# Third experts: rows fetched four tiles ahead, tile 0's small operations moved into the attention, eight buffers for scatter addresses and output weights

## The chip, the cores and the metric

One core of one Trainium2 chip runs the whole program in one launch. The metric is device time in microseconds; the time of a kernel is the median of its runs.

## The reference

The program is a network of four layers on an image of 256 channels and 64 x 64 = 4096 places (tokens), in float32. Layer 0 is a convolutional attention over boxes, layer 1 a deformable convolution, layer 2 a linear attention followed by a mixture of experts, layer 3 a full softmax attention followed by a mixture of experts. The change lies in the code of the two mixtures, which are called second experts (layer 2) and third experts (layer 3) here. The third one, cut to what is computed:

```python
gate_logits = xf @ Wg + bg                       # 4096 tokens, 8 experts
top_w, top_i = jax.lax.top_k(gate_logits, 2)
top_w = jax.nn.softmax(top_w, axis=-1)
w_dense = jnp.sum(one_hot(top_i, 8) * top_w[..., None], axis=1)
for e in range(8):
    h = jax.nn.gelu(xf @ W1[e] + b1[e])          # 256 -> 1024
    out = out + w_dense[:, e:e + 1] * (h @ W2[e] + b2[e])
```

The second mixture has the same form with a hidden size of 256.

## The kernel before

**Routing.** Each token goes to two experts only. `route` (L2028) handles a block of 512 tokens: it normalises them, computes logits, picks the two experts, counts, finds for each token its place in the list of each of its experts, and scatters the token's row of 260 numbers (256 channels, its number, its two weights, its first expert) by POOL's indirect DMAs into `xs` in memory (L2117, eight DMAs a block). `full_table` (L2125) and `tile_table` (L2157) then cut the lists into tiles of 256 rows: for each tile the expert, the first row, and masks. In layer 3 the first 20 tiles are taken from the counts before the last block (table A), and the other 16 from the final counts (table B). Three more tiles can follow under an If on a counter.

**One tile of experts** (`expert_tiles`, L2269):

- `load` calls `expert_load` (L2219): SP reads the tile's expert and first row from the table into registers and issues three DMAs: the rows of `xs` into `f_x` (260 KB; L2229 or L2235), and the two weight matrices (L2231, L2233). It runs `ahead` tiles before use: three in the second experts, two in the third. `f_x` has `ahead + 3` buffers.
- `turn` calls `expert_turn` (L2238): PE transposes the rows into PSUM (L2241), DVE copies them to `f_xT` (L2242).
- `where` (L2320) makes from the four extra numbers of each row the scatter addresses `f_at` and the weights `f_wgt` by nine small DVE operations (L2325 to L2333), each on two columns. Its five tags have four buffers each, so the `f_at` of a tile is written over the one of four tiles before, which a scatter may still be reading.
- `first` (L2296): PE's products into `f_h_ps` by the helper `mm` (L152), ACT's gelu into `f_h` (L2303).
- In the third experts `sides` (L2336) forms differences of the second weights on POOL (L2344), and `seven` (L2347) computes the second product as seven smaller ones, with DVE's sums around them (`f_hs` L2351 to L2354, `f_u` and `f_y` L2369 to L2373).
- `second` (L2375): DVE adds the bias to `f_y` (L2379 in the third experts, L2384 in the second), ACT scales it by `f_wgt` (L2386), and two POOL indirect DMAs scatter it to `ys` at the addresses in `f_at` (L2387). It is emitted one tile after `first`.

The loop at L2408 to L2422 emits, for tile i: the load of tile i + ahead, `first` of i, `turn` and `where` of i + 1, `second` of i - 1.

**The attention of layer 3** (`attn3`, L2483) runs over 8 blocks of 512 queries with 16 pairs of key tiles each. A round is `scores` (L2647: seven products on PE at L2653, DVE's sums of them at L2658 and in `together` at L2640 to L2643, ACT's exponential L2672, DVE's differences L2676 to L2678) and `values` (L2681, PE L2692) of two rounds before. Between rounds of a block stand the steps of the block before it: `finish` (L2701: the last product, DVE's `t` L2708) and the five steps of `route`. In the last block `full_table` and the `expert_load` of tile 0 are emitted in its round 9 (L2766 to L2770), and `expert_turn` of tile 0 in round 14 of 0 to 15 (L2771). The steps of the last block itself (four `finish`, five of `route`, then `tile_table`) are run inside the third experts' first tiles: `finish` between products of tile 0, the scatter into `xs` in tile 2, the table in tile 3.

**What sets the order.** Within `attn3` the order of PE and POOL is written out by hand; in the third experts that of PE, until the steps are used up. Everything else (DVE, ACT and SP in these stretches, and all engines in the second experts) is ordered by a scheduler when the program is built: it may move an operation of `where` of a later tile in front of one of an earlier tile. Each engine executes its list in order. A read of rows of `xs` that is emitted after a scatter into `xs` waits for that scatter.

Of the kernel before, what the change touches and what calls it, by code (L numbers as in the profile page):

```python
# [10 lines left out]
F32 = mybir.dt.float32  # L11
BF16 = mybir.dt.bfloat16
I32 = mybir.dt.int32
# [6 lines left out]
P = 128  # L20
C = 256
# [71 lines left out]
class Net:  # L93
# [30 lines left out]
    def weights(self, pool, names):  # L124

        for i, name in enumerate(names):
            src = self.A[name].rearrange("(k p) n -> p k n", p=P)
            w = pool.tile(list(src.shape), F32, tag=name, name=name)
            eng = self.nc.sync if i % 2 == 0 else self.nc.scalar
            eng.dma_start(out=w, in_=src)  # L130
            self.w[name] = w

    def rows(self, pool, first, last):

        lo, hi = PR[first].start, PR[last].stop
        pr = pool.tile([P, hi - lo], F32, tag=f"pr_{first}", name="pr", bufs=1)
        self.nc.scalar.dma_start(out=pr, in_=self.A["pr"][lo:hi].partition_broadcast(P))
        for name, at in PR.items():
            if lo <= at.start and at.stop <= hi:
                self.r[name] = pr[:, at.start - lo : at.stop - lo]  # L140
# [2075 lines left out]
            part = off[:, i : i + k, :].rearrange("p i k -> p (i k)")  # L2216
            nc.vector.scalar_tensor_tensor(part, self.nth[:, : k * NI], float(2 * N), part, ALU.add, ALU.mult)

    def expert_load(self, S, tab, j, x, w1, w2, rows_first):  # L2219
        nc, A, L = self.nc, self.A, S["L"]  # L2220
        why = "worked out from counts of tokens"
        e = nc.values_load(tab[0:1, 0, j : j + 1], engines=[mybir.EngineType.SP], min_val=0, max_val=(NE - 1) * P,
                           skip_runtime_bounds_check_because=why)
        row = nc.values_load(tab[0:1, 1, j : j + 1], engines=[mybir.EngineType.SP], min_val=0, max_val=NE * N - MT,
                             skip_runtime_bounds_check_because=why)
        src = self.xs[bass.ds(row, MT), :].rearrange("(i p) c -> p i c", p=P)
        x = x()
        if rows_first:
            nc.sync.dma_start(out=x, in_=src)  # L2229
        w1 = w1()  # L2230
        nc.sync.dma_start(out=w1, in_=A[f"f{L}_w1"][bass.ds(e, P), :])  # L2231
        w2 = w2()
        nc.sync.dma_start(out=w2, in_=A[f"f{L}_w2"][bass.ds(e, P), :])  # L2233
        if not rows_first:
            nc.sync.dma_start(out=x, in_=src)  # L2235
        return x, w1, w2

    def expert_turn(self, x, p, xT):  # L2238
        for k in range(2):
# [29 lines left out]
    def expert_tiles(self, S, order, wp, ps, steps, early, pre, written):  # L2269
        nc, A = self.nc, self.A  # L2270
        L = S["L"]
        tiles = range(len(order))
        of = lambda i, nm: S[order[i][0]][nm]
        hidden = 256 if L == 2 else 1024
        KH = hidden // P
        ahead = 3 if L == 2 else 2 if pre or not early else 1

        def load(i):
            if pre and i == 0:
                return pre["tile"]  # L2280
            lent = pre and i % 3 == 0
            pool = pre["pool"] if lent else wp
            kw = dict(bufs=1) if lent else dict(bufs=2) if early else {}
            return self.expert_load(
                S, of(i, "tab"), order[i][1],
                lambda: wp.tile([P, NI, CX], F32, tag="x", name="f_x", bufs=ahead + 3),
                lambda: pool.tile([P, 2 * hidden + KH], F32, tag="w1", name="f_w1", **kw),
                lambda: pool.tile([P, KH * C + C], F32, tag="w2", name="f_w2", **kw),
                i > 0,
            )  # L2290

        def turn(x):
            p = ps.tile([P, 2, MT], F32, tag="x", name="f_x_ps", bufs=1 if early else 2)
            return self.expert_turn(x, p, wp.tile([P, 2, MT], F32, tag="xT", name="f_xT", bufs=3))
# [23 lines left out]
            return h  # L2318

        def where(i, x):  # L2320

            tl = lambda tag, dt=F32: wp.tile([P, NI], dt, tag=tag, name="f_" + tag, bufs=4)
            first, second, to, wgt, at = tl("first"), tl("second"), tl("to"), tl("wgt"), tl("at", I32)
            op, j = nc.vector, order[i][1]
            op.tensor_scalar(first, x[:, :, C + 3], of(i, "ex")[:, j : j + 1], None, ALU.is_equal)  # L2325
            op.tensor_scalar(second, first, -1.0, 1.0, ALU.mult, ALU.add)
            op.tensor_tensor(wgt, second, x[:, :, C + 2], ALU.mult)
            op.tensor_scalar(second, second, float(N), None, ALU.mult)
            op.tensor_tensor(to, x[:, :, C], second, ALU.add)
            op.tensor_tensor(to, to, of(i, "in")[:, j, :], ALU.mult)  # L2330
            op.tensor_tensor(at, to, of(i, "off")[:, j, :], ALU.add)
            op.tensor_tensor(first, first, x[:, :, C + 1], ALU.mult)
            op.tensor_tensor(wgt, wgt, first, ALU.add)  # L2333
            return at, wgt

        def sides(w2):  # L2336

# [58 lines left out]
                    written.close()  # L2396

        nc.scalar.activation(wp.tile([P, 1], F32, tag="g", name="f_gelu", bufs=1), self.one, AF.Gelu)
        ld = {i: load(i) for i in tiles[:ahead]}
        if pre:  # L2400
            for f in pre["ahead"][:1]:
                f()
            xT = pre["xT"]
        else:
            xT = turn(ld[tiles[0]][0])
        to = where(tiles[0], ld[tiles[0]][0])
        done = None
        for i in tiles:  # L2408
            if i + ahead <= tiles[-1]:
                ld[i + ahead] = load(i + ahead)  # L2410
            x, w1, w2 = ld.pop(i)
            h = first(xT, w1, (pre["ahead"][1:] if i == 0 else ()) if steps else None)
            now = (i, h, w2, sides(w2)) + to
            step()
            if i < tiles[-1]:
                xT = turn(ld[i + 1][0])
                to = where(i + 1, ld[i + 1][0])
            if done is not None:
                second(*done)
                step()  # L2420
            done = now
# [61 lines left out]
    def attn3(self, t, S):  # L2483
# [6 lines left out]
        with (  # L2490
# [28 lines left out]
            if True:  # L2519
# [6 lines left out]
                def bank(few=False):  # L2526
                    banks.append(banks.pop(0))
                    return (keep_ps if banks[-1] == "q" else ps).tile([P, NB], F32, tag=banks[-1], name="a3_q_ps")
# [172 lines left out]
                def finish(b, i):  # L2701
                    o = bank()[:, : C + 1]
                    at = oTs[b].rearrange("p m h n -> p m (h n)")[:, :, i * P : (i + 1) * P]
                    self.mm(o, [(at[:, kt, :], wvp[:, kt, :]) for kt in range(2)])
                    ti = b * TPB + i
                    r = S["r"][:, ti : ti + 1]
                    nc.vector.reciprocal(r, o[:, C : C + 1])
                    nc.vector.scalar_tensor_tensor(t[:, ti, :], o[:, :C], r, t[:, ti, :], ALU.mult, ALU.add)  # L2708
# [41 lines left out]
                with tc.manual_schedule(engines={ET.PE, ET.Pool}):  # L2750
                    steps = iter(())
                    for g in range(first, G + LAG):
                        if g < G:
                            scores(g)
                        values(g - LAG)
                        if g + 3 < G:
                            fetch(g + 3)
                        b, j = divmod(g - LAG, NPAIR)
                        if b > 0:
                            if j < TPB:  # L2760
                                finish(b - 1, j)
                            elif j == TPB:
                                steps = route((b - 1) * TPB, TPB)
                            elif j % 2 == 0 or b == NBLK - 1:
                                next(steps, None)
                            if b == NBLK - 1 and j == TPB + 5:  # L2766
                                self.full_table(S, keep, bank)
                                one = lambda shape, tag: keep.tile([P] + shape, F32, tag=tag, name="f_" + tag, bufs=1)
                                tile = self.expert_load(S, S["A"]["tab"], 0, lambda: one([NI, CX], "x"), lambda: one([16 * P + 8], "w1"),
                                                        lambda: one([9 * C], "w2"), True)  # L2770
                            if b == NBLK - 1 and j == NPAIR - 2:  # L2771
                                xT = self.expert_turn(tile[0], bank().rearrange("p (k n) -> p k n", k=2), one([2, MT], "xT"))
            left.close()
            last = route((NBLK - 1) * TPB, TPB)
            go = lambda: next(last, None)
            self.experts(
                S, [go] * 5 + [lambda: self.tile_table(S, keep, bank, True)],
                {"pool": keep, "tile": tile, "xT": xT, "ahead": [lambda i=i: finish(NBLK - 1, i) for i in range(TPB)]},
            )

    def limits3(self, S, pool):
# [252 lines left out]
```

## Time and profile before

| | us |
|---|---|
| median of 3 runs (3406.99 to 3415.58) | 3408.2 |
| the profiled execution | 3404.69 |
| its span, first to last instruction | 3402.8 |

The stretches of the span that the change touches, with the busy time of the engines, in us:

| stretch | what runs | PE | DVE | ACT | POOL | DMA share |
|---|---|---|---|---|---|---|
| 1746 to 1922 | second experts | 156.4 | 88.3 | 64.0 | 69.0 | 0.77 |
| 2795 to 2831 | last rounds of the attention of layer 3 | 35.2 | 25.6 | 8.4 | 8.4 | 0.33 |
| 2831 to 3360 | third experts | 503.4 | 289.4 | 177.7 | 279.2 | 0.51 |

The mean granted clock of TensorE over the span was 0.958. A line of the waits gives who waited, for whom (`<-`), the sum in us, how often and the longest; a line of the order of time gives start and duration in us, engine, line, operation, result and operands, the number of instructions, and in brackets the idle time of the engine just before, with what ended it. SPq is SP's queue of DMA issues.

### The profile page before, as it was taken

To read this page: it belongs to the slowest core of one execution; us is meant where nothing else is said; L and a number is where in the kernel's file an instruction comes from. 1 tells how busy PE (TensorE), PEld (TensorE's weight loads), DVE (VectorE), ACT (ScalarE), POOL (GpSimd) and SP (SyncE) were. 2 spreads that over 40 slices of the span, in tenths; PEclk is the share of its full clock that TensorE was granted. 3 is DMA by queue.
4 is the path that set the end of the run, shared out by engine and by line. 5 is a ranking of instruction groups with operands and counts; after the bars stand their busy time and mean duration, and the time that the engine had idled before them with its cause. 6 is when DMAs were issued, how large, how long until landed. Compare 5 with 4: busy or idle time off the path is not lost.

```text
span 3402.8 us, 66193 instructions
## 1 busy us (share of the span) xinstructions
PE 3095.0 (91%) x25774; PEld 2314.3 (68%) x25774; DVE 2299.0 (68%) x5331; ACT 1329.1 (39%) x2552; POOL 1460.9 (43%) x1318
## 2 busy tenths in 40 slices
PE   6789999999977899797969789999999999899997
PEld 3343444344435888766857567888888888789996
DVE  8885677577764777787855576777777776555552
ACT  4444343434425666343633352322222223333331
POOL 2028787878842555433444353000000013555552
PEclk9889999999988999898979899999999999999998
DMA  1145555521134122200158553223332224555554
GB/s 72 42 109 147 159 153 156 155 66 52 46 107 127 57 75 75 58 1 2 54 186 262 190 212 118 90 96 100 100 99 100 81 95 165 184 201 208 203 204 176
DMA packets 241688, 407.01 MB, mean 120 GB/s; under 512 B 78353, under 2 KB 152850, under 8 KB 231890
## 3 DMA queue, kind: packets, MB, share of 16 engines
q1 hardware_dynamic: 212002, 344.40, 31.7%
q0 software_dynamic: 13056, 35.93, 2.8%
q10 hardware_dynamic: 16304, 22.31, 2.0%
q8 instruction: 207, 3.39, 0.4%
q14 instruction: 119, 0.97, 0.1%
HBM read 287.07 MB, written 111.30 MB: 117 GB/s over the span
## 4 chain that ended last, share of the span: by engine, by line
PE 41%; DVE 8%; DMA 5%; issue 4%; ACT 3%; POOL 3%; SPq 0%; POOLq 0%; DVEq 0%; ACTq 0%
PE a_sa_ps L2653 6%; PE f_h_ps L152 6%; PE a_oa_ps L2692 3%; PE a_ob_ps L2692 3%; DMA ys<-f_y,f_at 3%; PE a_oc_ps L2692 3%; PE a_sb_ps L2653 3%; PE f_ya_ps L152 3%; PE l_acc_ps L1160 2%; PE f_yb_ps L152 2%; POOL ys L2387 2%; PE a_od_ps L2692 1%; PE a_q_ps L152 1%; PE a_sc_ps L2653 1%; PE a_qkv_ps L152 1%
## 5 line engine op out<-in xcount | busy, mean ns | idle before, releaser
L776 ACT COPY l_sc<-l_s 128x384 f32<-128x384 f32 (+1 forms) x632 | 304.0, 532 | 452.3 <-PE l_s L769 446.2
L781 DVE TENSOR_TENSOR l_sm<-l_s,mask 128x256 f32<-128x256 f32 (+2 forms) x628 | 308.1, 551 | 90.4 <-PE l_s L769 89.2
L152 PE MATMUL f_h_ps<-f_xT,f_w 128*128 128x256 f32 x1440 | 342.2, 388 | 29.1 <-ACT f_h L2303 19.0
L2117 POOL DMA_INDIRECT xs<-f_room,f_to x64 | 64.3, 1005 | 641.9 <-DVE a_e L2640 474.9
L152 PEld LDWEIGHTS f_h_ps<-f_xT,f_w 128*128 128x128 f32 x1440 | 262.7, 192 | 92.3 <-ACT f_h L2303 42.2
L769 PE MATMUL l_s<-l_q,l_k 32*128 32x256 f32 (+3 forms) x2944 | 270.5, 453 | 0.0
L2672 ACT ACTIVATE a_e<-a_e 128x512 f32<-128x512 f32 x256 | 156.2, 630 | 245.2 <-DVE a_e L2642 240.9
L786 POOL TENSOR_TENSOR l_sm<-l_sc,mask 128x768 f32<-128x768 f32 (+1 forms) x116 | 202.5, 1754 | 87.8 <-ACT l_sc L776 87.7
L2303 ACT ACTIVATE f_h<-f_h_ps,f_w 128x256 f32<-128x256 f32 x360 | 164.8, 470 | 178.7 <-PE f_h_ps L152 178.5
L1156 DVE TENSOR_TENSOR l_pr<-l_vk,l_w_ps 128x1280 f32<-128x1280 f32 x128 | 186.6, 1482 | 54.2 <-PE l_acc_ps L1160 35.0
L769 PEld LDWEIGHTS l_s<-l_q,l_k 32*128 32x128 f32 x2944 | 132.4, 183 | 115.2 <-issue 67.5
L2387 POOL DMA_INDIRECT ys<-f_y,f_at x144 | 147.8, 1027 | 146.2 <-ACT f_y L2386 115.9
L1160 PE MATMUL l_acc_ps<-ident,l_pr 128*128 128x128 f32 x1600 | 197.9, 278 | 6.5 <-POOL l_pr L1151 6.2
L1160 PEld LDWEIGHTS l_acc_ps<-ident,l_pr 128*128 128x128 f32 x1600 | 184.5, 144 | 13.3 <-POOL l_pr L1151 8.2
L790 POOL TENSOR_TENSOR l_sm<-l_sc,mask 128x256 f32<-128x256 f32 (+1 forms) x220 | 185.1, 869 | 15.3 <-ACT l_sc L776 14.4
L2344 POOL TENSOR_TENSOR f_wt<-f_w 128x512 f32<-128x512 f32 x72 | 90.1, 1272 | 225.0 <-PE f_ya_ps L152 201.1
L2653 PE MATMUL a_sa_ps<-a_q,a_kt 128*128 128x256 f32 x512 | 156.2, 387 | 15.6 <-DVE a_u L2658 14.7
L2657 ACT COPY a_u<-a_sa_ps 128x256 f32<-128x256 f32 x128 | 47.6, 372 | 293.7 <-PE a_sa_ps L2653 293.6
L2653 PE MATMUL a_sa_ps<-a_qt,a_kt 128*128 128x256 f32 x512 | 153.6, 382 | 0.0
L815 PE MATMUL l_b_ps<-l_sm,l_v 128*32 128x256 f32 (+2 forms) x2176 | 153.5, 372 | 0.0
L786 POOL TENSOR_TENSOR l_sm<-l_sc,mask_c 128x768 f32<-128x768 f32 (+1 forms) x64 | 122.3, 1929 | 36.5 <-ACT l_sc L776 36.0
L2692 PE MATMUL a_ob_ps<-a_et,a_vs 128*128 128x256 f32 x512 | 132.2, 381 | 0.0
(590 smaller groups left out, 7272.4 us busy)
## 6 DMA issues: line engine op xcount, KB each, us to landing
a_kt<-a_kd SPq DMA_DIRECT2D x128, 512.0 KB
f_w<-in_f_w SPq DMA_DIRECT2D x36, 1152.0 KB
f_w<-in_f_w SPq DMA_DIRECT2D x36, 1028.0 KB
xs<-zero SPq DMA_DIRECT2D x8, 4160.0 KB
l_vk<-vt SPq DMA_DIRECT2D x180, 128.0 KB
f_x<-xs SPq DMA_DIRECT2D x72, 260.0 KB
f_w<-in_f_w SPq DMA_DIRECT2D x36, 384.0 KB
l_rcp<-l_recd SPq DMA_DIRECT2D x48, 256.0 KB
```

Of the source, the lines that this page charges most:

```text
L152: self.nc.tensor.matmul(out, lhsT, rhs, start=(i == 0), stop=(i == len(pairs) - 1))
L769: nc.tensor.matmul(s[pair, j][:, at : at + m, :], key(hp), qs[hp], start=(z == 0), stop=(z == len(pieces) - 1))
L776: nc.scalar.copy(sc[:, j], s[1, j])
L781: nc.vector.tensor_tensor(to(pair, j, kind, at), pick(s[pair, j], kind, which), mask, ALU.mult)
L786: nc.gpsimd.tensor_tensor(out[:, :, at, :], of[:, :, which, :], bc(mask, 1, 2), ALU.mult)
L790: nc.gpsimd.tensor_tensor(to(1, j, kind, at), pick(sc[:, j], kind, which), mask, ALU.mult)
L1156: nc.vector.tensor_tensor(pr, vk, bc(held["w"][:, j, dy], 3, D), ALU.mult)
L1160: nc.tensor.matmul(acc[:, m, j, :], pf[:, dx, m * P : (m + 1) * P], self.ident, is_transpose=True, start=(j == 0 and dy == 0 and dx == 0 a ...
L2303: nc.scalar.activation(h[:, m, :], p[:, m % 2, :], AF.Gelu, bias=w1[:, 2 * hidden + m : 2 * hidden + m + 1])
L2387: nc.gpsimd.indirect_dma_start(out=self.ys_parts[(i % 4) * NI + k], in_=y[:, k, :], in_offset=None, out_offset=bass.IndirectOffsetOnAxis(a ...
L2653: mm = lambda out, i, right: nc.tensor.matmul(out, A[i], right, start=True, stop=True)
L2692: nc.tensor.matmul(out, vs[:, j, i, :], right, start=(j == 0 and side != 1), stop=(j == NPAIR - 1 and side != 0))
```

## The change

It has three parts.

1. `expert_load` is split into `expert_rows` and `expert_weights`. With `pre` (the third experts' 36 tiles) rows are fetched four tiles ahead (`ahead_x = ahead + 2`, seven buffers of `f_x` instead of five), weights still two. In the second experts both stay three ahead.
2. `where` becomes the method `expert_where`. That of tile 0 of the third experts is emitted beside `expert_turn` in the attention, into buffers of its own, instead of at the start of `expert_tiles`.
3. The five tags of `where` have eight buffers instead of four, in the second experts as well as in the third.

```diff
@@ -2216,24 +2216,37 @@
             part = off[:, i : i + k, :].rearrange("p i k -> p (i k)")
             nc.vector.scalar_tensor_tensor(part, self.nth[:, : k * NI], float(2 * N), part, ALU.add, ALU.mult)
 
-    def expert_load(self, S, tab, j, x, w1, w2, rows_first):
-        nc, A, L = self.nc, self.A, S["L"]
-        why = "worked out from counts of tokens"
-        e = nc.values_load(tab[0:1, 0, j : j + 1], engines=[mybir.EngineType.SP], min_val=0, max_val=(NE - 1) * P,
-                           skip_runtime_bounds_check_because=why)
-        row = nc.values_load(tab[0:1, 1, j : j + 1], engines=[mybir.EngineType.SP], min_val=0, max_val=NE * N - MT,
-                             skip_runtime_bounds_check_because=why)
-        src = self.xs[bass.ds(row, MT), :].rearrange("(i p) c -> p i c", p=P)
-        x = x()
-        if rows_first:
-            nc.sync.dma_start(out=x, in_=src)
+    def expert_at(self, tab, k, j, most):
+        return self.nc.values_load(tab[0:1, k, j : j + 1], engines=[mybir.EngineType.SP], min_val=0, max_val=most,
+                                   skip_runtime_bounds_check_because="worked out from counts of tokens")
+
+    def expert_rows(self, tab, j, x):
+        row = self.expert_at(tab, 1, j, NE * N - MT)
+        self.nc.sync.dma_start(out=x, in_=self.xs[bass.ds(row, MT), :].rearrange("(i p) c -> p i c", p=P))
+        return x
+
+    def expert_weights(self, L, tab, j, w1, w2):
+        nc, A = self.nc, self.A
+        e = self.expert_at(tab, 0, j, (NE - 1) * P)
         w1 = w1()
         nc.sync.dma_start(out=w1, in_=A[f"f{L}_w1"][bass.ds(e, P), :])
         w2 = w2()
         nc.sync.dma_start(out=w2, in_=A[f"f{L}_w2"][bass.ds(e, P), :])
-        if not rows_first:
-            nc.sync.dma_start(out=x, in_=src)
-        return x, w1, w2
+        return w1, w2
+
+    def expert_where(self, T, j, x, tl):
+        first, second, to, wgt, at = tl("first"), tl("second"), tl("to"), tl("wgt"), tl("at", I32)
+        op = self.nc.vector
+        op.tensor_scalar(first, x[:, :, C + 3], T["ex"][:, j : j + 1], None, ALU.is_equal)
+        op.tensor_scalar(second, first, -1.0, 1.0, ALU.mult, ALU.add)
+        op.tensor_tensor(wgt, second, x[:, :, C + 2], ALU.mult)
+        op.tensor_scalar(second, second, float(N), None, ALU.mult)
+        op.tensor_tensor(to, x[:, :, C], second, ALU.add)
+        op.tensor_tensor(to, to, T["in"][:, j, :], ALU.mult)
+        op.tensor_tensor(at, to, T["off"][:, j, :], ALU.add)
+        op.tensor_tensor(first, first, x[:, :, C + 1], ALU.mult)
+        op.tensor_tensor(wgt, wgt, first, ALU.add)
+        return at, wgt
 
     def expert_turn(self, x, p, xT):
         for k in range(2):
@@ -2270,23 +2283,27 @@
         nc, A = self.nc, self.A
         L = S["L"]
         tiles = range(len(order))
-        of = lambda i, nm: S[order[i][0]][nm]
+        tab = lambda i: (S[order[i][0]]["tab"], order[i][1])
         hidden = 256 if L == 2 else 1024
         KH = hidden // P
         ahead = 3 if L == 2 else 2 if pre or not early else 1
-
-        def load(i):
+        ahead_x = ahead + 2 if pre else ahead
+
+        def rows(i):
             if pre and i == 0:
-                return pre["tile"]
+                return pre["x"]
+            return self.expert_rows(*tab(i), wp.tile([P, NI, CX], F32, tag="x", name="f_x", bufs=ahead_x + 3))
+
+        def weights(i):
+            if pre and i == 0:
+                return pre["w"]
             lent = pre and i % 3 == 0
             pool = pre["pool"] if lent else wp
             kw = dict(bufs=1) if lent else dict(bufs=2) if early else {}
-            return self.expert_load(
-                S, of(i, "tab"), order[i][1],
-                lambda: wp.tile([P, NI, CX], F32, tag="x", name="f_x", bufs=ahead + 3),
+            return self.expert_weights(
+                L, *tab(i),
                 lambda: pool.tile([P, 2 * hidden + KH], F32, tag="w1", name="f_w1", **kw),
                 lambda: pool.tile([P, KH * C + C], F32, tag="w2", name="f_w2", **kw),
-                i > 0,
             )
 
         def turn(x):
@@ -2318,20 +2335,8 @@
             return h
 
         def where(i, x):
-
-            tl = lambda tag, dt=F32: wp.tile([P, NI], dt, tag=tag, name="f_" + tag, bufs=4)
-            first, second, to, wgt, at = tl("first"), tl("second"), tl("to"), tl("wgt"), tl("at", I32)
-            op, j = nc.vector, order[i][1]
-            op.tensor_scalar(first, x[:, :, C + 3], of(i, "ex")[:, j : j + 1], None, ALU.is_equal)
-            op.tensor_scalar(second, first, -1.0, 1.0, ALU.mult, ALU.add)
-            op.tensor_tensor(wgt, second, x[:, :, C + 2], ALU.mult)
-            op.tensor_scalar(second, second, float(N), None, ALU.mult)
-            op.tensor_tensor(to, x[:, :, C], second, ALU.add)
-            op.tensor_tensor(to, to, of(i, "in")[:, j, :], ALU.mult)
-            op.tensor_tensor(at, to, of(i, "off")[:, j, :], ALU.add)
-            op.tensor_tensor(first, first, x[:, :, C + 1], ALU.mult)
-            op.tensor_tensor(wgt, wgt, first, ALU.add)
-            return at, wgt
+            tl = lambda tag, dt=F32: wp.tile([P, NI], dt, tag=tag, name="f_" + tag, bufs=8)
+            return self.expert_where(S[order[i][0]], order[i][1], x, tl)
 
         def sides(w2):
 
@@ -2396,25 +2401,34 @@
                     written.close()
 
         nc.scalar.activation(wp.tile([P, 1], F32, tag="g", name="f_gelu", bufs=1), self.one, AF.Gelu)
-        ld = {i: load(i) for i in tiles[:ahead]}
+        xs, ws = {}, {}
+        for i in tiles[:ahead_x]:
+            if pre or i > 0:
+                xs[i] = rows(i)
+            if i < ahead:
+                ws[i] = weights(i)
+            if i not in xs:
+                xs[i] = rows(i)
         if pre:
-            for f in pre["ahead"][:1]:
-                f()
-            xT = pre["xT"]
+            pre["ahead"][0]()
+            xT, to = pre["xT"], pre["to"]
         else:
-            xT = turn(ld[tiles[0]][0])
-        to = where(tiles[0], ld[tiles[0]][0])
+            xT = turn(xs[tiles[0]])
+            to = where(tiles[0], xs[tiles[0]])
         done = None
         for i in tiles:
+            if i + ahead_x <= tiles[-1]:
+                xs[i + ahead_x] = rows(i + ahead_x)
             if i + ahead <= tiles[-1]:
-                ld[i + ahead] = load(i + ahead)
-            x, w1, w2 = ld.pop(i)
+                ws[i + ahead] = weights(i + ahead)
+            w1, w2 = ws.pop(i)
+            xs.pop(i)
             h = first(xT, w1, (pre["ahead"][1:] if i == 0 else ()) if steps else None)
             now = (i, h, w2, sides(w2)) + to
             step()
             if i < tiles[-1]:
-                xT = turn(ld[i + 1][0])
-                to = where(i + 1, ld[i + 1][0])
+                xT = turn(xs[i + 1])
+                to = where(i + 1, xs[i + 1])
             if done is not None:
                 second(*done)
                 step()
@@ -2766,16 +2780,19 @@
                             if b == NBLK - 1 and j == TPB + 5:
                                 self.full_table(S, keep, bank)
                                 one = lambda shape, tag: keep.tile([P] + shape, F32, tag=tag, name="f_" + tag, bufs=1)
-                                tile = self.expert_load(S, S["A"]["tab"], 0, lambda: one([NI, CX], "x"), lambda: one([16 * P + 8], "w1"),
-                                                        lambda: one([9 * C], "w2"), True)
+                                tab = S["A"]["tab"], 0
+                                pre = {"pool": keep, "x": self.expert_rows(*tab, one([NI, CX], "x")),
+                                       "w": self.expert_weights(3, *tab, lambda: one([16 * P + 8], "w1"), lambda: one([9 * C], "w2"))}
                             if b == NBLK - 1 and j == NPAIR - 2:
-                                xT = self.expert_turn(tile[0], bank().rearrange("p (k n) -> p k n", k=2), one([2, MT], "xT"))
+                                pre["xT"] = self.expert_turn(pre["x"], bank().rearrange("p (k n) -> p k n", k=2), one([2, MT], "xT"))
+                                tl = lambda tag, dt=F32: keep.tile([P, NI], dt, tag="e" + tag, name="f_" + tag, bufs=1)
+                                pre["to"] = self.expert_where(S["A"], 0, pre["x"], tl)
             left.close()
             last = route((NBLK - 1) * TPB, TPB)
             go = lambda: next(last, None)
             self.experts(
                 S, [go] * 5 + [lambda: self.tile_table(S, keep, bank, True)],
-                {"pool": keep, "tile": tile, "xT": xT, "ahead": [lambda i=i: finish(NBLK - 1, i) for i in range(TPB)]},
+                {**pre, "ahead": [lambda i=i: finish(NBLK - 1, i) for i in range(TPB)]},
             )
 
     def limits3(self, S, pool):
```

## The prediction

> **What bounds the kernel now.** I read the page first (busy time, the span in slices), then the two stretches that the diff touches: the second experts at 1746–1922 us and the third at 2795–3360, each by its waits, then by the order of time on DVE, PE and SP. The page:
>
> ```profile
> PE 3095.0 (91%) x25774; PEld 2314.3 (68%) x25774; DVE 2299.0 (68%) x5331; ACT 1329.1 (39%) x2552; POOL 1460.9 (43%) x1318
> ...
> PE   6789999999977899797969789999999999899997
> PEclk9889999999988999898979899999999999999998
> ```
>
> PE is busy for 91%, so only PE's gaps in the touched stretches can be won: a DVE wait that leaves no PE gap is worth nothing. The diff gives eight buffers to both expert stages, since both call the same function, so the second experts belong to the case. Their waits (engine, line, waited for, us, times, longest):
>
> ```profile
> DVE f_at L2331 <- DMA ys<-f_y,f_at: 56.2, 30, 4.3
> ...
> PE f_h_ps L152 <- DVE f_xT L2242: 8.0, 9, 2.3
> ...
> PE f_h_ps L152 <- ACT f_h L2303: 1.6, 4, 0.6
> ```
>
> DVE stands 56.2 us waiting to overwrite an address buffer whose scatter of four tiles before has not landed; f_xT, behind it in DVE's queue, is what PE waits for. PE's share by stretches (us, then busy of PE, PEld, DVE, ACT, POOL, clock, DMA share, GB/s):
>
> ```profile
> 1800.00:1840.00 40.00, 38.72 (x182) 30.16 (x183) 21.00 (x98) 15.67 (x36) 17.95 (x19) 1.00 0.84 268
> 1840.00:1880.00 40.00, 35.77 (x168) 27.36 (x166) 20.52 (x92) 14.41 (x33) 16.53 (x17) 1.00 0.84 270
> ```
>
> PE idles 1.3 and 4.2 us in these two. The third experts, from 2831 on:
>
> ```profile
> DVE f_at L2331 <- DMA ys<-f_y,f_at: 37.4, 26, 2.9
> ...
> PE f_h_ps L152 <- ACT f_h L2303: 17.4, 10, 9.9
> ...
> PE a_q_ps L152 <- DVE t L2708: 2.0, 1, 2.0
> ```
>
> Two single places matter there. One is DVE, then PE, near 2900:
>
> ```profile
> 2900.09 0.59 DVE L2325 TENSOR_SCALAR f_first<-f_x,f_exA 128x2 f32<-128x2 f32 x1 [10.23 <-DMA f_x<-xs]
> ```
> ```profile
> 2906.86 3.78 PE L152 MATMUL f_h_ps<-f_xT,f_w 128*128 128x256 f32 x8 [9.91 <-ACT f_h L2303]
> ```
>
> f_first of tile 5 holds DVE for 10.23 us for rows that SP issues only at 2897.30, after the last scatter into xs; f_y of tile 2 stands behind it, ACT's gelus behind that, PE behind those. The other is the place that tile 0's small operations will get, in DVE's and SP's order:
>
> ```profile
> 2807.28 0.69 DVE L2641 TENSOR_TENSOR a_u<-a_sb_ps,a_u 128x512 f32<-128x512 f32 x1
> 2808.01 0.42 DVE L2642 TENSOR_TENSOR a_e<-a_u,a_sb_ps 128x256 f32<-128x256 f32 x1
> ```
> ```profile
> 2811.76 0.39 SPq L2229 DMA_DIRECT2D f_x<-xs  x1
> ```
>
> **What the Trainium skill says.** "TensorE: Matmul & The Clock Gate", Architectural detail, calls ACT and DVE strict FIFOs: nothing passes a waiting instruction. The 10.23 us above agree. The same page, Part 1, What's actually happening, has the clock fall to half after an idle window of about 3.4 us; the trace agrees: the eight matmuls after the 9.91 us gap take 3.78 us, eight without one (at 2831.21) 1.89. "DMA: Bandwidth & Descriptors", Rules for kernel authors, says that a DMA which reads what another wrote is issued only after the first one's completion; the trace agrees (last scatter issued 2894.6, landing 2.5 median, rows issued 2897.30).
>
> **Part 1, eight buffers, second experts.** f_at of a tile now waits for the scatter eight tiles back, over 16 us older at 4 us a tile, so the 56.2 us go whole. What is it on PE? SP issues the rows of tile 6 at 1763.07 and of tile 35 at 1897.32: 134.25 / 29 = 4.63 us a tile. Undisturbed tiles stand 4.07 apart (1776.66 to 1780.73). Excess: 29 x 0.56 = 16 us; that is the upper end. PE's own rows say 8.0 + 1.6 = 9.6. What is late next is the rows: the order of the changed kernel puts f_first of a tile ahead of f_y of the tile four before, some 4.5 us after its rows' issue at that pace (my reading of both orders). Before, f_first came 5.0 to 8 us after the issue and waited twice only, at the start, when it landed in 4.4 and 5.7; alone, 2.8 (2897.30 to 2900.09). Bytes at 4.07 us rise to 268 x 4.63 / 4.07 = 305 GB/s, below the 320 to 338 that the best slices of the stage show. So small new waits: I take -10.5, ends 0 and -16.
>
> **Part 1, third experts.** The same wait, 37.4 us on DVE, reaches PE in the 17.4 us row: 9.9 are the stall near 2900, 2.2 the table loads at 2845, the rest 1.83 at 2951 and seven of 0.49, 17.4 - 9.9 - 2.2 = 5.3. A tile takes 13.6 us, a scatter 6.4 to land, so nothing waits eight tiles back. -5.3; ends -3 and -5.3.
>
> **Part 2, rows four tiles ahead.** Per tile one row load of 260 KB moves up SP's order; the number of loads (36 tiles, each one of rows and two of weights) stays. At the start rows of tiles 2 to 4 stand before the weights of tile 2: two more than before, 520 KB at the 400 GB/s that this stretch reached = 1.3 us later; those weights are used a tile (13.6 us) later: 0. If that cover were gone, 1.3 us once. And the stall? The first rows emitted after the last scatter are now tile 7's, not tile 5's. But the scheduler moves f_first along by the same two tiles: in the changed order f_first of tile 7 stands where tile 5's stood, after L2188 and before f_u and f_y of tile 2. The stall keeps its place and length: 0; ends 0 and -12 (9.9 plus the 1.9 of slow clock).
>
> **Part 3, tile 0's nine operations in the attention.** At the start of the experts DVE runs them ahead of t, four beside POOL's f_wt:
>
> ```profile
> 2830.91 1.13 DVE L2326 TENSOR_SCALAR f_second<-f_first 128x2 f32<-128x2 f32 x1
> 2832.08 1.18 DVE L2327 TENSOR_TENSOR f_wgt<-f_second,f_x 128x2 f32<-128x2 f32 x1
> ...
> 2834.48 0.47 DVE L2708 SCALAR_TENSOR_TENSOR t<-a_q_ps,f_r,t 128x256 f32<-128x256 f32 x1
> ```
> ```profile
> 2835.09 1.11 PE L152 MATMUL a_q_ps<-a_wvp,a_oT 128*128 128x257 f32 x4 [1.99 <-DVE t L2708]
> ```
>
> Taken away, PE wins its 1.99 and part of the 3.48 - 1.89 = 1.6 of slow clock that follow: -2.5, ends -2.0 and -3.6. Against it stands a new wait. In the changed order f_first of tile 0 comes directly after the a_u that ran at 2807.28 and before the a_e of 2808.01. Its rows are issued at 2811.76 and land 2.8 us later, at 2814.5. So DVE holds for 6.5 us. Behind it stand that a_e and the next (0.42 and 0.68), which free the banks that PE writes next: PE comes to them at 2810.97 and gets them near 2815.9, a gap of 4.9. That is over the 3.4 us window, so up to 1.7 of slow clock may follow. I take +5.5; ends 0 (if the scores have cover that I don't see) and +6.7. The other eight (0.15 to 0.2 each, 1.4 together) lie in DVE's gaps of 0.5 to 0.7 in each round: 0.
>
> **Sum.** -10.5 - 5.3 + 0 - 2.5 + 5.5 = -12.8. The profiled execution took 3404.7 (span 3402.8, 1.9 around it): 3391.9. The median shown, 3408.2, is 3.5 above that execution; on it, 3395.4. I predict 3395.
>
> **Rivals.**
> A. Rows are there early after all: the stall near 2900 goes too. For it: fetching earlier is what a late row asks for. Against: the order. 3395 - 11 = 3384. Chance 0.12.
> B. DMA takes the place of f_at in the second experts: rows come late on a fuller queue, and 0 to 3 us are won there. For: share 0.84 at 268 GB/s already. Against: 338 in single slices. 3395 + 9 = 3404. Chance 0.22.
> C. Slower: in the second experts the landing grows past the old cushion. f_first stands earlier, before f_y and f_xT; landing 6.5 us instead of 4.5 makes 2.0 of DVE wait, about 0.9 hidden, 1.1 on PE a tile: 5.18 us a tile, 31 x 0.55 = +17. With -5.3 - 2.5 + 5.5 = -2.3 from the rest: 3408 + 15 = 3423. It ends slower from a landing of about 6.4 us (5.04 a tile, +12.7 - 2.3 = +10.4). For: 5.7 was seen at the start. Against: 5.0 without a wait later. Chance 0.08.
> D. My likeliest: 0.58.
>
> **How the numbers follow.** Of the ends, the second experts weigh most: with 0 or -16, 3406 or 3390; attention and start move it by 5 at most. 3382 to 3407 takes in A, B and D, leaving C and the tails. A measurement tells 0.3% from no change: 10.2 us, so faster ends below 3398.0. D lies there with two chances in three (0.39), A wholly (0.12), B hardly (0.01): 0.52. C: 0.08 slower. Same: 0.40. D alone: 3388 to 3402.
>
> **What would show it.** f_at waits of DVE: near 0 in both stages. Rows of the second experts issued 4.2 to 4.4 us apart. An f_first wait near 10 us still before f_y of tile 2, PE resuming 9 to 10 us late. A new f_first wait of 6 us in the attention near 2808 (less what was won before) and PE's gap of 5 after it. No PE wait for t at the start. I am wrong if f_first waits take over in the second experts, if that stall moves or goes, or if PE's gap in the attention is missing.

## The result and the profile after

The changed kernel takes 3394.1 us (median of 6 runs, 3392.0 to 3397.9), the kernel before 3409.3 (median of 6, 3407.0 to 3415.6): a ratio of 0.9952, interval 0.9939 to 0.9965, some 15 us less. The prediction was 3395. The span of the profiled executions went from 3402.8 to 3390.5, 12.3 us; the sum of the prediction was -12.8. That the total fits doesn't mean that its terms do: part of the fit is luck, as the account of its steps shows. I divided both spans at five instructions which PE and DVE run in both (first transpose of the second experts, first product of the attention's weights, the last sum into `a_oT` of block 6 and of block 7, last product of the third experts); each row runs from the start of one to the start of the next:

| stretch, us | before | after | difference |
|---|---|---|---|
| up to the second experts | 1751.8 | 1752.1 | +0.3 |
| second experts | 168.7 | 154.6 | -14.1 |
| attention up to block 6's end | 811.6 | 810.5 | -1.1 |
| last block of the attention | 97.8 | 105.3 | +7.5 |
| third experts | 522.8 | 516.7 | -6.1 |
| tail | 50.1 | 51.3 | +1.2 |

**Second experts.** In the waits of the changed kernel from 1746 to 1912 there is no `f_at` any more (56.2 us before); DVE waits for rows instead, in 27 of the 36 tiles, and PE hardly waits at all:

```profile
DVE f_first L2240 <- DMA f_x<-xs: 31.0, 27, 4.8
...
PE f_h_ps L152 <- ACT f_h L2320: 1.8, 2, 1.3
PEld f_h_ps L152 <- DVE f_xT L2255: 0.8, 3, 0.3
```

PE's share in stretches (us, busy of PE, PEld, DVE, ACT, POOL, clock, DMA share, GB/s):

```profile
1800.00:1840.00 40.00, 39.93 (x197) 32.43 (x195) 25.12 (x108) 17.34 (x40) 19.25 (x20) 1.00 0.91 285
1840.00:1880.00 40.00, 38.74 (x192) 31.48 (x191) 24.70 (x104) 16.28 (x39) 17.60 (x19) 1.00 0.95 306
```

So 31 us of DVE's waits took the place of 56, and PE, idle for 1.3 and 4.2 us here before, now idles 0.1 and 1.3. Rows are issued 4.18 us apart (1763.65 to 1880.63, 28 intervals), not 4.63.

**Attention.** The order of time of DVE, PE and SP near 2800:

```profile
2792.36 0.69 DVE L2655 TENSOR_TENSOR a_u<-a_sb_ps,a_u 128x512 f32<-128x512 f32 x1
2799.57 0.23 DVE L2240 TENSOR_SCALAR f_first<-f_x,f_exA 128x2 f32<-128x2 f32 x1 [6.52 <-DMA f_x<-xs]
2799.71 0.41 DVE L2656 TENSOR_TENSOR a_e<-a_u,a_sb_ps 128x256 f32<-128x256 f32 x1
```
```profile
2800.77 1.22 PE L2667 MATMUL a_sa_ps<-a_q,a_kt 128*128 128x256 f32 x2 [4.56 <-DVE a_e L2657]
```
```profile
2796.78 0.39 SPq L2225 DMA_DIRECT2D f_x<-xs  x1
```

An operation on two columns, 0.23 us long, stands between `a_u` and `a_e`, waits 6.52 us for rows that SP issued only at 2796.78, and PE misses 4.56 us. After that the granted clock (third column from the end) is at half:

```profile
2801.00:2806.00 5.00, 5.00 (x12) 3.98 (x13) 3.40 (x12) 0.75 (x2) 0.00 (x0) 0.50 0.74 310
```

The round's scores take from 2800.77 to 2806.60, 5.8 us, against 3.0 before (2810.97 to 2813.99). 4.56 + 2.8 is 7.4 of the 7.5 in the table.

**Third experts.** Here are PE's waits from 2795 to 3360, and the two lines of the stall after the last scatter:

```profile
PE f_h_ps L152 <- ACT f_h L2320: 9.1, 2, 8.1
...
PE f_h_ps L152 <- issue: 4.8, 1, 4.8
PE a_sa_ps L2667 <- DVE a_e L2657: 4.6, 1, 4.6
```
```profile
2893.83 0.60 DVE L2240 TENSOR_SCALAR f_first<-f_x,f_exA 128x2 f32<-128x2 f32 x1 [8.40 <-DMA f_x<-xs]
```
```profile
2900.61 3.78 PE L152 MATMUL f_h_ps<-f_xT,f_w 128*128 128x256 f32 x8 [8.08 <-ACT f_h L2320]
```

The eight short waits behind `f_at` (5.3 us) are gone. The stall is still there: it belongs to tile 7's rows now and costs PE 8.08 instead of 9.91. PE's wait of 1.99 us for `t` is gone, but before the next group of products stands one of 1.16. The profile puts it down to `f_to`, which ended 0.07 us after the next `t`:

```profile
2829.46 1.11 PE L152 MATMUL a_q_ps<-a_wvp,a_oT 128*128 128x257 f32 x4 [1.16 <-DVE f_to L2245]
```

And PE has a new gap of 4.8, from what DVE does beside POOL at that time:

```profile
2836.68 1.19 DVE L2241 TENSOR_SCALAR f_second<-f_first 128x2 f32<-128x2 f32 x1
...
2837.98 1.23 DVE L2247 TENSOR_TENSOR f_first<-f_first,f_x 128x2 f32<-128x2 f32 x1
...
2839.34 0.68 DVE L2255 COPY f_xT<-f_x_ps 128x512 f32<-128x512 f32 x1
```
```profile
2836.58 2.61 POOL L2349 TENSOR_TENSOR f_wt<-f_w,f_wt 128x512 f32<-128x512 f32 x2
```
```profile
2834.72 0.60 PE L2254 MATMUL f_x_ps<-ident,f_x 128*128 128x128 f32 x4
2840.12 8.83 PE L152 MATMUL f_h_ps<-f_xT,f_w 128*128 128x256 f32 x32 [4.79 <-issue]
```

Small operations of tile 2 stand ahead of `f_xT` of tile 1, and three of them take over a microsecond each, as three of tile 0 did before. The 32 products then run in 8.83 us instead of 7.14. The place in the queue is not new. In the kernel before, the same operations of tile 2 stood ahead of the same copy, but POOL's differences ended at 2846.03, and all but the first of them ran after that, in 0.2 us each:

```profile
2843.43 2.60 POOL L2344 TENSOR_TENSOR f_wt<-f_w,f_wt 128x512 f32<-128x512 f32 x2
```
```profile
2844.64 0.60 PE L2241 MATMUL f_x_ps<-ident,f_x 128*128 128x128 f32 x4
```
```profile
2846.10 0.17 DVE L2326 TENSOR_SCALAR f_second<-f_first 128x2 f32<-128x2 f32 x1
...
2846.66 0.69 DVE L2242 COPY f_xT<-f_x_ps 128x512 f32<-128x512 f32 x1
```

Counted from the first product of `t` that waits for the last `a_oT` (2830.67 before, 2823.28 after), PE comes to tile 1's transposes at 11.4 instead of 14.0, 2.5 us sooner. POOL's pairs, which wait for the weights of tile 1, start at 10.8 against 10.2, so they now run beside tile 2's operations. `f_xT` is copied at 16.1, against 16.0 before: the 2.5 us are lost again, and the slower products come on top.

### The profile page after: what moved, and what is told of

Read it like the earlier page. It is cut to its first block, busy times and chain, and to the rows that moved or that the text cites. A ratio compares the mean times of both kernels' runs of the same rounds, so it can differ in the third digit from the quotient of the medians.

```text
span 3390.5 us, 66220 instructions
## 1 busy us (share of the span) xinstructions
PE 3089.0 (91%) x25774; PEld 2316.8 (68%) x25774; DVE 2300.9 (68%) x5331; ACT 1330.4 (39%) x2552; POOL 1460.4 (43%) x1318
## 4 chain that ended last, share of the span: by engine, by line
PE 47%; DVE 8%; DMA 4%; ACT 3%; issue 3%; POOL 2%; SPq 0%; POOLq 0%; DVEq 0%; ACTq 0%
PE f_h_ps L152 8%; PE a_sa_ps L2667 6%; PE f_ya_ps L152 3%; PE l_acc_ps L1160 3%; PE a_oa_ps L2706 3%; PE a_ob_ps L2706 3%; PE a_oc_ps L2706 3%; PE a_sb_ps L2667 3%; PE f_yb_ps L152 3%; DVE l_pr L1156 2%; PE a_q_ps L152 1%; PE a_od_ps L2706 1%; PE a_sc_ps L2667 1%; DMA ys<-f_y,f_at 1%; PE a_qkv_ps L152 1%
## 5 line engine op out<-in xcount | busy, mean ns | idle before, releaser
L2667 PE MATMUL a_sb_ps<-a_qt,a_kt 128*128 128x256 f32 x512 | 132.3, 381 | 0.0
```

Source lines behind the costliest of these rows:

```text
L2667: mm = lambda out, i, right: nc.tensor.matmul(out, A[i], right, start=True, stop=True)
```

## The experiments

When the first four were run, the kernel before took 3444 us, and 3404 to 3406 with the others; so ratios count, each against before in the same session, and beside them the stretches, which are those of one execution each. How far single executions differ can be read from the second experts: with four buffers and the scheduler's order they took 164.9 to 168.7 us in four profiles, with eight 151.7 to 154.6 in seven. So a difference of some 3 us in that stretch shows nothing.

### Each part alone

```diff
-            tl = lambda tag, dt=F32: wp.tile([P, NI], dt, tag=tag, name="f_" + tag, bufs=4)
+            tl = lambda tag, dt=F32: wp.tile([P, NI], dt, tag=tag, name="f_" + tag, bufs=8)
```

> The kernel before with eight buffers for the five tags of the small operations, in both expert stages; rows and tile 0 as before. Theory (the gain is the eight buffers alone, and the move of tile 0's operations costs 7.5 us): the second experts end 14 us earlier, the third lose their 5.3 us of PE waits for f_at, nothing is lost in the attention, so about 3389 us, 20 below before and 5 below the changed kernel. Rival (the buffers help only together with the early rows and the move, which let the small operations stand earlier): 3397 or more, no better than the changed kernel.

Measured: 0.9932 (0.9917 to 0.9947), 23 us below before. Second experts 152.7, last block of the attention 97.8, third experts 515.0. By the medians the buffers alone win more than the whole change; the two intervals overlap, but the last block, which has lost nothing here, accounts for the difference.

The next run has eight buffers in the third experts only:

```diff
+            tl = lambda tag, dt=F32: wp.tile([P, NI], dt, tag=tag, name="f_" + tag, bufs=4 if L == 2 else 8)
```

> Eight buffers in the third experts only, four in the second, the rest as before. Theory: only the 5.3 us of PE waits behind f_at go, 3404 us; the second experts keep their 56 us of f_at waits and 4.6 us a tile. Rival (in the third experts the new place of the small operations matters, not the buffers): 3408 to 3409, no change.

Measured: 0.9976 (0.9968 to 0.9985), 8 us. Second experts 165.6, third 514.3. So of the gain of the buffers about 8 lie in the third experts (5 to 11 by the interval, which holds the 5.3 forecast), and the rest in the second. The profiled execution was the fastest of twelve, 12 us below their median, so its stretches may be short.

Then come the early rows alone, written as the changed kernel without its other two parts:

```diff
-            tl = lambda tag, dt=F32: wp.tile([P, NI], dt, tag=tag, name="f_" + tag, bufs=8)
+            tl = lambda tag, dt=F32: wp.tile([P, NI], dt, tag=tag, name="f_" + tag, bufs=4)
...
-            xT, to = pre["xT"], pre["to"]
+            xT, to = pre["xT"], where(0, pre["x"])
...
-                                pre["to"] = self.expert_where(S["A"], 0, pre["x"], tl)
```

> Rows four tiles ahead in the third experts and nothing else: four buffers, tile 0's small operations at the start of the experts as before. Theory (the scheduler moves f_first along with the rows): the wait of 8 to 10 us before f_y of tile 2 stays, 3409 to 3412 us. The rows of tile 1 to 4 at the start may cost 1 to 3 us. Rival (early rows take that stall away): f_first has no wait over 3 us there and the time is near 3398.

Measured: 1.0297 (1.0284 to 1.0311), 103 us slower; third experts 624.5. Neither theory had this. The waits from 2795 on, and one tile in DVE's order:

```profile
DVE f_at L2246 <- DMA ys<-f_y,f_at: 217.8, 32, 8.3
...
PE f_h_ps L152 <- ACT f_h L2320: 68.3, 26, 4.6
```
```profile
3150.05 0.16 DVE L2246 TENSOR_TENSOR f_at<-f_to,f_offA 128x2 int32<-128x2 f32 x1 [6.74 <-DMA ys<-f_y,f_at]
3150.13 0.69 DVE L2356 TENSOR_TENSOR f_hs<-f_h 128x512 f32<-128x512 f32 x1
```

The rows are there earlier, so the scheduler puts the small operations earlier, until `f_at` comes right behind the scatter which still holds its buffer: POOL issued the last two at 3142.2 and 3143.5, and DVE stands for 6.74 us ahead of `f_hs`. So it goes in every tile from tile 4 on (32 waits). Early rows need the eight buffers; the gain of the buffers doesn't need the rows.

The last part alone is the move of tile 0's operations (four buffers as above, and rows two tiles ahead):

```diff
-        ahead_x = ahead + 2 if pre else ahead
+        ahead_x = ahead
```

> Tile 0's small operations in the attention and nothing else: four buffers, rows two tiles ahead. Theory (f_first holds DVE for rows that have not landed): PE loses 4.6 us plus 2 to 3 of slow clock in the last rounds of the attention, and wins 2 to 3.6 at the start of the experts: 3412 to 3414 us, slower than before. Rival (the loss in the changed kernel comes from elsewhere, such as the rows queued on SP): 3406 to 3408, faster than before by the 2 us at the start.

Measured: 1.0021 (1.0014 to 1.0027), 7 us slower, where 3 to 5 were expected. Last block 105.6, third experts 520.7; DVE's gap is the same, PE's 4.56 too.

### The change with one part undone

Tile 0's operations back at the start of the experts:

```diff
-            xT, to = pre["xT"], pre["to"]
+            xT, to = pre["xT"], where(0, pre["x"])
...
-                                pre["to"] = self.expert_where(S["A"], 0, pre["x"], tl)
```

> The changed kernel without its third part: tile 0's small operations at the start of the experts as before; eight buffers and rows four tiles ahead stay. Theory (the move costs 7.5 us in the attention and wins nothing that lasts at the start, because the operations of tiles 1 and 2 take the place of tile 0's): last block of the attention 97.8 us, experts 515 to 518, ratio 0.9925 to 0.9935, 6 to 8 us below the changed kernel. Rival (the move wins the 2 to 3.6 us at the start that were forecast): experts 519 or more, 4 us or less won.

Measured: 0.9936 (0.9919 to 0.9953), against 0.9952 for the change. The intervals overlap, so the stretches decide: last block 97.8, third experts 515.9 (with the move 516.7). The move wins nothing in the experts.

Rows two tiles ahead again, with the eight buffers and the move:

```diff
-        ahead_x = ahead + 2 if pre else ahead
+        ahead_x = ahead
```

> The changed kernel with rows fetched two tiles ahead instead of four (eight buffers and the move of tile 0's operations stay). Theory (the early rows themselves are a loss of about 4 us at the start of the third experts, since the small operations of tiles 2 to 4 then stand ahead of f_xT of tile 1): experts at 513 us instead of 516.7, about 4 us less than the changed kernel, ratio 0.994. Rival (early rows win something or are free): the same as the changed kernel, 0.995, or above it.

Measured: 0.9953 (0.9939 to 0.9966), experts 516.0. My theory fell: the early rows cost nothing in sum. PE's stall after the scatter is 9.89 with rows two ahead and 8.08 with four (-1.8), and the start, from the first product of `t` to the 32 products' end, takes 24.8 against 25.7 (+0.9); both are single executions.

### The order on DVE alone

`issue_after` fixes only the place of instructions in their engine's queue: what is traced under it is queued behind the instruction named. First the changed kernel with tile 0's operations queued behind the last differences of the scores:

```diff
-                    eng.tensor_tensor(et[:, 3], e[:, 3], et[:, 2], ALU.subtract)
+                    self.last_et = eng.tensor_tensor(et[:, 3], e[:, 3], et[:, 2], ALU.subtract)
...
-                                pre["to"] = self.expert_where(S["A"], 0, pre["x"], tl)
+                                with tc.issue_after(self.last_et.ins):
+                                    pre["to"] = self.expert_where(S["A"], 0, pre["x"], tl)
```

> The changed kernel with one edit: tile 0's small operations are queued on DVE behind the last round's differences a_et, some 8 us after their rows have landed. Theory (f_first waiting in DVE's queue is all of the loss in the attention): the last block of the attention takes 97.8 us again instead of 105.3, the rest is as in the changed kernel, so 7 to 8 us less than the changed kernel: a ratio to before of 0.993. Rival (the nine operations or the earlier table work cost something themselves): less than 4 us won, ratio 0.9945 or more.

Measured: 0.9943 (0.9927 to 0.9958). The last block takes 97.8 again and the experts 516.5; the interval holds both expectations, so it is the stretch that decides: the loss in the attention is that one wait.

Then, instead, the small operations of tile i are queued behind `f_y` of tile i - 4 (`ys` holds the additions that finish `f_y`):

```diff
-                to = where(i + 1, xs[i + 1])
+                if pre and i >= 3:
+                    with self.tc.issue_after(ys.pop(i - 3).ins):
+                        to = where(i + 1, xs[i + 1])
...
```

> The changed kernel with one edit: from tile 4 on the small operations of tile i are queued on DVE behind f_y of tile i - 4, so that f_first of tile 7 comes after f_y of tile 3 and no longer ahead of f_y of tile 2. Theory (the stall of 8 to 10 us after the last scatter is an operation that stands too early, not a row that comes too late): PE loses its gap of 8.1 us there and 1.9 of slow clock, so 10 us less than the changed kernel, ratio 0.9925. Rival (the stall moves on to f_xT of tile 5 or to the next wait): 0 to 3 us won, ratio 0.995.

Measured: 0.9938 (0.9926 to 0.9950); experts 512.6, 4 us less, not 10. `f_first` no longer waits there, but PE still misses 4.21. The order of time of DVE, then of POOL, shows what came in its place:

```profile
2884.73 4.25 DVE L2207 TENSOR_TENSOR f_skip<-f_skip,f_tau 128x19 f32<-128x19 f32 x1
```
```profile
2885.21 2.50 POOL L2349 TENSOR_TENSOR f_wt<-f_w 128x512 f32<-128x512 f32 x2
2887.67 2.61 POOL L2349 TENSOR_TENSOR f_wt<-f_w,f_wt 128x512 f32<-128x512 f32 x2
```

A table operation on 19 columns, 0.17 us elsewhere, takes 4.25 beside POOL's differences, and `f_y` of tile 2 stands behind it. The Trainium skill's "GPSIMD Engine Reference", Key points, says that GpSimd shares its SBUF interfaces with VectorE and contends with its instructions of two SBUF inputs or in a 2-port perf mode; this operation has two inputs, so that fits, though no run here takes the two engines apart. So the rival that the stall moves on was half right.

The next run changes the order alone, in both expert stages, with four buffers and rows two ahead; `turned` is the copy to the tile's own `f_xT`, and tile 0's operations stand behind the last `a_et` as above:

```diff
-                to = where(i + 1, xs[i + 1])
+                with self.tc.issue_after(self.turned.ins):
+                    to = where(i + 1, xs[i + 1])
```

> No part of the change except the place of tile 0's operations, which are queued behind the last a_et; four buffers, rows two tiles ahead. Instead, in both expert stages the small operations of a tile are queued on DVE behind its own f_xT, one tile ahead of use, so that they never stand in front of work that is due earlier. Theory (all of these waits come from the order on DVE, not from too few buffers or late rows): no f_at wait over 1 us in either stage, no stall after the last scatter, 14 + 8 + 2 + 10 = 34 us less than before, ratio 0.990. Rival (four buffers are too few in themselves): the f_at waits stay in the second experts, where a scatter takes longer than a tile, and the gain is 12 us or less, ratio 0.9965.

Measured: 0.9897 (0.9883 to 0.9910), 35 us below before. Second experts 154.3, last block 97.9, third experts 500.5. In the second experts some `f_at` waits are left, up to 2.9 us where none over 1 was expected, and they hardly reach PE; in the third there are none, and from 2890 to 3300 PE has no gap (the columns as above):

```profile
DVE f_at L2246 <- DMA ys<-f_y,f_at: 7.9, 10, 2.9
PE f_h_ps L152 <- ACT f_h L2320: 3.4, 4, 1.7
```
```profile
2890.00:3300.00 410.00, 410.00 (x2768) 376.37 (x2767) 226.23 (x605) 144.49 (x331) 233.32 (x182) 1.00 0.56 204
```

The third experts' gain of 22.3 us is accounted for to within 1 us: the start takes 19.6 instead of 23.9, the stall of 9.9 with 1.9 of slow clock after it is gone, and so are the 5.3 behind `f_at`. Four buffers were not too few, and the rows all but on time: the small operations stood too early.

Then the same order stands on top of the whole change (the edit is against the run before):

```diff
-            tl = lambda tag, dt=F32: wp.tile([P, NI], dt, tag=tag, name="f_" + tag, bufs=4)
+            tl = lambda tag, dt=F32: wp.tile([P, NI], dt, tag=tag, name="f_" + tag, bufs=8)
...
-        ahead_x = ahead
+        ahead_x = ahead + 2 if pre else ahead
```

> The changed kernel (eight buffers, rows four tiles ahead, tile 0's operations in the attention) with the queueing on DVE of the run before: the small operations of each tile behind its own f_xT, those of tile 0 behind the last a_et. Theory (once the order is right, neither more buffers nor earlier rows have anything left to win): the same as that run with four buffers and rows two ahead, ratio 0.9885 to 0.991. Rival (the buffers still save the 8 us of f_at waits that were left in the second experts, or the rows the last waits in the third): 4 us or more below it, ratio under 0.9885.

Measured: 0.9881 (0.9862 to 0.9900). The ratio lies just on the rival's side and its interval holds both. Second experts 155.5, so the buffers show no gain there though the `f_at` waits are gone; third 498.6: the early rows take away one last wait of PE for rows of 1.55 us. Here too PE has no gap from 2890 to 3300:

```profile
2890.00:3300.00 410.00, 410.00 (x2769) 376.45 (x2768) 224.79 (x601) 145.13 (x333) 235.75 (x184) 1.00 0.55 199
```

In the last run the order is set in the third experts only:

```diff
-                with self.tc.issue_after(self.turned.ins):
+                with self.tc.issue_after(self.turned.ins) if pre else ExitStack():
```

> As the run before with all three parts and the queueing on DVE, but the queueing only in the third experts; the second experts keep the changed kernel's own order with eight buffers. Theory (in the second experts eight buffers and the better order are two ways to the same end, and the former came out 2 to 3 us shorter there: 152 to 153.5 against 154.3 and 155.5): second experts 152 to 153.5, the rest equal, ratio 0.987 to 0.988. Rival (the difference there was noise between executions): 154 to 155.5, ratio 0.988 to 0.989.

Measured: 0.9887 (0.9870 to 0.9903); second experts 152.6, as the theory said, but 3 us are within what single executions of this stretch differ by, and the ratio doesn't tell it from the run before. The last three beat both kernels clearly (3364 to 3372 us); which of them is best stays open.

## Why the prediction was right or wrong, by its steps

- **Eight buffers, second experts: right in mechanism, short in size.** -10.5 said, -14.1 measured (over all profiles with the scheduler's order, those with eight buffers lie some 14 below those with four). The waits of PE in the profile (9.6) were too low a guide, the excess of the tiles' period (16) the better one. I had taken off for rows that land late: they do, 31 us on DVE, but nearly all of it in time that DVE had to spare. So one sign of being wrong came true by its words, `f_first` waits took over, and yet cost next to nothing; the sign should have been a wait of PE. Rival B is out: DMA share rose to 0.95, and PE's waits for `f_h` came to 1.8 us.
- **Eight buffers, third experts: right.** -5.3 said; the waits are gone, and the stretch's -6.1 without what changed at the stall (-1.8) and at the start (+1.7) is -6.0.
- **Early rows: right.** 0 said. The stall kept its place for the reason given, that `f_first` moves along with the rows; its 1.8 us less and 0.9 more at the start nearly cancel. Rival A is out. What I overlooked is how much this depends on the buffers (103 us without them).
- **Tile 0's operations, start: wrong.** -2.5 said. By the trace of the change the start is 1.7 us longer (23.9 to 25.7 us up to the end of the 32 products). Up to tile 1's transposes the forecast holds: PE is 2.5 us sooner there. It waits 1.16 us in place of 1.99, because `f_first` of tile 1 waits 1.17 us for its rows ahead of the next `t`, and no slow clock follows. The step that failed is taking that win as kept: I asked for the cost of the operations that go, not for what the earlier PE would meet next. It meets tile 2's operations while POOL's `f_wt` runs beside them, and the clock falls after the gap of 4.8. Alone, with four buffers and later rows, the move won about 1 us there (22.8).
- **Tile 0's operations, attention: right in mechanism, short in size.** DVE's wait 6.52 (6.5 said), PE's gap 4.56 (4.9). The slow clock after it cost 2.8; I had given it 1.7 at most and 0.6 in the value taken. Measured +7.5 against +5.5. Nor are the 3.4 us that the prediction goes by the least gap that brings it: in the kernel before, eight products after a gap of 1.99 us took 3.48 us instead of 1.89, at a clock of 0.50, while after one of 2.21 us at 2847.45 it stayed full.
- **Sum.** 3.6 us more won in the second experts, 4.2 us less at the start, 2.0 us more lost in the attention, 1.8 us won at the stall: errors of both signs that cancelled. The terms were right in kind but for the start; that they sum to within 1 us is luck. Rival C is out: the landing did grow past the cushion at times (6.6 us from issue to `f_first` once), and PE lost next to nothing by it.

What none of my rivals had is the common cause. The waits for buffers, for rows after the scatter and for rows in the attention are one thing, and the run of the order alone shows it: an operation of 0.2 us that isn't due yet stands in an in-order queue ahead of one that is due, with an operand or a buffer that isn't ready. The change treated the symptom at one place (a buffer to wait for), left it at another (the rows) and added it at a third (the attention).

## What to carry to other kernels

When a trace shows a small operation waiting long, ask first what stands behind it in its engine's queue and when its result is needed; moving it back may be worth more than making its operand earlier. If operands come earlier and a scheduler orders the queue, read where it puts the operation then. And when a change lets one engine come sooner, see what the others are doing at the moment that it then meets.

## What was not expected of the hardware

- A DVE operation on 19 columns took 4.25 us beside two pairs of POOL's subtractions (0.17 elsewhere), and one of 38 columns 4.28 in the run with everything combined, where PE had no gap behind it. That one reads a single tile, so if POOL is the cause, two inputs are not needed for it:

```profile
2875.14 4.28 DVE L2213 TENSOR_SCALAR f_offB<-f_inB 128x38 f32<-128x38 f32 x1
```

- After a PE gap of 4.56 us the next 14 products took 5.8 us instead of 3.0, at a granted clock of 0.50. The loss by the clock was over half of the gap itself.
